# A residual chain of modulated 1-d convolutions: R's sums of the first iteration in the new order on VectorE, and the tap differences behind that iteration's tables

## The chip, the cores and the metric

The kernel runs on one core of a Trainium2 chip. The metric is the device time of one execution in microseconds (us); each kernel is run several times, and the median counts. The engines are called by the profile's names: PE is TensorE's matmul side and PEld its weight loads, DVE is VectorE, ACT is ScalarE, POOL is GpSimd, SP is SyncE, which issues most DMAs.

## The reference

A batch of 128 sequences x[b] (64 channels, 1024 positions) is run through four layers, and the result is added to x. Each layer scales its weights by a style of the batch element, normalises them (the demodulation) and convolves:

```python
def _layer(x, style, w, b, mw, mb, typ):
    s = style @ mw.T + mb
    weight = SCALE * w * s[:, None, :, None]
    demod = lax.rsqrt(jnp.sum(weight * weight, axis=(2, 3)) + EPS)
    weight = weight * demod[:, :, None, None]
    if typ == 'same':          out = conv_same(x, weight) + b
    elif typ == 'upsample':    out = blur(conv_up(x, weight) + b, 2 * k, (1, 1))
    elif typ == 'downsample':  out = conv_down(blur(x, k, (2, 2)), weight) + b
    return out
out = x
for i, typ in enumerate(('same', 'upsample', 'same', 'downsample')):
    out = _layer(out, style, weights[i], biases[i], mod_w[i], mod_b[i], typ)
return x + out
```

All weights are 64 x 64 x 3, the blur is (1, 3, 3, 1)/8, everything is float32.

## The kernel before, in words

Inside the sequence the four layers and the two blurs are one linear map from 64 to 64 channels, so the kernel multiplies the weights of all layers together for each batch element (the weight chain), and then convolves x once with the product. The batch is worked in groups of four elements, numbered q = 0 to 31: two on the two halves of the 128 partitions, times two on the free axis.

The weight chain of a group has four steps. `scale3` scales the last layer's taps (tile wd, ScalarE). `stage1` multiplies them by layer 2 into S. `stage2` multiplies S by the blurred taps E of the upsampling layer; the sums stand in PSUM as psR, and ScalarE copies them, scaled by the table tC, into R, slots 0 to 6. `stage3` multiplies R by layer 0 into Wf, the nine taps of the whole map. `combine_a` and `combine_b` then build sums of taps (tile H) on VectorE. The convolution itself is split, with such sums of taps and of input planes (tiles G and T), into five products, `conv0` to `conv4` (all at L754, into the PSUM tiles psA and Y). `sum1`, `sum2` and ScalarE's `output` put the results together, and SP's queue stores them. G and T come from the loaded planes X: `in_g01`, `in_g2`, `in3` and `in04` on VectorE, `in1` and `in2` on GpSimd for most groups.

The order of work is written out by hand. Every engine takes its instructions strictly in the order of the program text, and waits at the first one whose operands are not there. A preparation and four `early_turn`s (q = 0 to 3) come first; from q = FIRST = 4 on, `turn_of(q)` is used to near the end, and three groups are finished by hand. Turn q finishes group q and prepares n = q + 1 (combinations, first products), c = q + 2 (stages 2 and 3) and s = q + 4 (stage 1). The turn q = 4, the entry, has an order of its own, since it takes over from the early turns. The turns also carry small work at fixed places, in the lists EXTRA (early turns), TABLES and SIDE (later turns): tables of scales for the groups that follow, bias vectors, the ends of the sequences.

In `turn_of`, stage 3 is in two halves. `stage3_b` has seven products into the next psA; the last of them reads the slots 7 and 8 of R, which are two sums of other slots of R and are made by `r_sums` (L587 to L589). Its result goes by ScalarE to psW and to Wf. `stage3_a` has the other products, into psW, some of them with differences of taps in the place of taps.

From q = 5 on, stage 2 of group q + 3 is begun by `share` and finished a turn later in `stage2_rest`, which reads differences of E's taps (Ed, which lie in the tile wsq). `tap_differences` (L454 to L459) makes these with three GpSimd subtractions, once, in the list EXTRA at the end of turn 3. GpSimd's next work is the `r_sums` of turn 4, and behind it turn 4's tables, `table_C`, `vector_c2` and `vector_Da`.

Of the kernel before, what the change touches and what calls it, by code (L numbers as in the profile page):

```python
# [63 lines left out]
def kernel(  # L64
# [18 lines left out]
    nc_v, nc_a, nc_g = nc.vector, nc.scalar, nc.gpsimd  # L83
# [191 lines left out]
    def table(eng, t, bs, upper, lower, src, mul):  # L275

        qs = slice(bs.start // 4, bs.stop // 4)
        for rows, sel in ((T, upper), (Bo, lower)):
            sel = sel if isinstance(sel, tuple) else (sel,)
            n = 2 // len(sel)  # L280
            for i, s in enumerate(sel):
                v = src.rearrange("c (q s) -> c q s", s=4)[rows, :, s]
                dst = t[rows, qs, n * i : n * (i + 1)]
                if isinstance(mul, float):
                    eng.tensor_scalar_mul(dst, v, mul)
                else:
                    m = mul.rearrange("c (q s) -> c q s", s=4)[rows, :, s]
                    eng.tensor_mul(dst, v, m)
# [16 lines left out]
    def table_C(bs, eng=nc_g):  # L305
        table(eng, tC, bs, slice(0, 2), slice(2, 4), dm[:, 1, bs], dm[:, 0, bs])

    def table_3(bs):
        table(nc_g, t3, bs, ALT, ODD, dm[:, 3, bs], var[:, 3, bs])
        table(nc_g, td, bs, slice(0, 2), slice(2, 4), dm[:, 3, bs], 1.0)  # L310
# [143 lines left out]
    def tap_differences():  # L454

        d = Ed[:, :4].rearrange("c (a b) o -> c a b o", a=2)
        for b in range(2):
            nc_g.tensor_sub(d[:, :, b], E[:, 4 * b : 4 * b + 5 : 4], E[:, 2:7:4])  # L458
        nc_g.tensor_sub(Ed[:, 4:], E[:, 3:8:4], E[:, 5:6].to_broadcast([P, 2, C]))  # L459
# [62 lines left out]
    def stage2(q, pool=None, engs=(nc_a, nc_a), between=None):  # L522
        st = chain[q]
        shared = q in shared_ps
        ps = stage2_rest(q) if shared else unit(pool or ps_w, f"psR{q}")
        for n, e in enumerate(() if shared else (-2, -1, 0, 1, 2, 3, 4, 5, 6)):
            if e % 2 == 0:
                a, lo, m = slice(1, 4), e // 2 + 1, 3
            else:
                a, lo, m = slice(4, 6), (e + 3) // 2, 2  # L530
            for r, rows in enumerate(HALF):
                for c, cols in enumerate(HALF):
                    src = st[c if r == 0 else 1 - c]
                    nc.tensor.matmul(  # L534
                        ps[r][cols, lo * C : (lo + m) * C],
                        E[rows, e + 2, :],
                        src[rows, a, :],
                        start=(n == 0),
                        stop=(n == 8),
                        skip_group_check=True,  # L540
                    )
        if between:
            between()
        t = r_pool.tile([P, 2, 9, C], F32, tag="R", name=f"R{q}")
        for r in range(2):
            scaled_copy(engs[r], flat(t[:, r, :7]), ps[r][:, : 7 * C], tC[:, q, r : r + 1])
        chain[q] = t
        return ps
# [35 lines left out]
            src = ps[r][:, : n * C].rearrange("c (a o) -> c a o", o=C)  # L584
            scaled_copy(engs[r], W[:, at : at + n, r], src, t0[:, q, r : r + 1])

    def r_sums(q):  # L587
        t = chain[q]
        nc_g.tensor_add(t[:, :, 7:9], t[:, :, 2:6:3], t[:, :, 3:7:3])  # L589

    shared_w = {}

# [62 lines left out]
    def residual(q):  # L655

        W = Wq[q][0]
        for r in range(2):
            v = W[:, tap(1, 1), r, :]
            nc_v.scalar_tensor_tensor(v, idn3, t3[:, q, r : r + 1], v, op0=ALU.mult, op1=ALU.add)  # L660

    def sum_of(out, x, f, y, op=ALU.add):
        nc_v.scalar_tensor_tensor(out, x, f, y, op0=ALU.mult, op1=op)  # L663

    def taps(q):
        W, H_ = Wq[q]
        merged = (*(W[:, i] for i in TAPS), *(H_[:, i] for i in range(3)))
        return [t.rearrange("c g r o -> c g (r o)") for t in merged]

    def combine_a(q):  # L670

        chain.pop(q)
        a, b, c, h1, h2, h3 = taps(q)
        sum_of(h1, c, -2.0, a)
        residual(q)
        sum_of(h3, h1, 1.0 / 6.0, b)
# [52 lines left out]
    def in2(q, eng):  # L729
        if q < NQ:  # L730
            t, g = t_tile(q, "T12"), Gs[q]
            eng.tensor_sub(t[:, :, 1, :NJ], plane(g, 2), plane(g, 1))  # L732
# [10 lines left out]
    def product(q, m, ps, groups=range(K)):  # L743

        W, H_ = Wq[q]
        tag, i = SLOT[m]
        for g in groups:
            for s, rows in enumerate(HALF):
                for c, cols in enumerate(HALF):
                    if m in (0, 4):  # L750
                        w = W[rows, tap(m // 2, g), c, :]
                    else:
                        w = H_[rows, m - 1, g, c, :]
                    nc.tensor.matmul(  # L754
                        ps[s][cols, :NB],
                        w,
                        Ts[q, tag][rows, c, i, g : g + NB],
                        start=(g == 0 and m == 3),
                        stop=(g == K - 1),
                        skip_group_check=True,  # L760
                    )
# [42 lines left out]
    def conv2(q, *groups):  # L804
        product(q, 2, banks(q), groups or range(K))

    def sum2(q, steps=(0, 1)):
        if 0 in steps:
            m3 = m3c.pop(q)
            for s, a in enumerate(banks(q)):  # L810
                sum_of(Y[:, s, :NB], m3[:, s], 3.0, a[:, :NB])
        for s, a in parts(q) if 1 in steps else ():
            nc_v.tensor_sub(y1w[q][:, s], y1w[q][:, s], a)  # L813

    def conv4(q, *groups):
        product(q, 4, Y_banks, groups or range(K))

    def conv0(q, *groups):
        product(q, 0, banks(q), groups)
# [60 lines left out]
    def vector_Da(bs):  # L880
        nc_g.tensor_mul(Da[:, bs], sc[:, 3, bs], dm[:, 2, bs])

    def with_bias(dst, v, l, bs):
        n = bs.stop - bs.start
        nc_g.tensor_mul(dst[:, bs], v[:, bs], bb[:, l : l + 1].to_broadcast([P, n]))

    def vector_c0(bs):
        with_bias(c0f, dm[:, 1], 0, bs)
# [4 lines left out]
    def vector_c2(bs):  # L893
        with_bias(c2f, sc[:, 3], 2, bs)
# [318 lines left out]
    REST = PART[2]  # L1213
# [32 lines left out]
    def layers(i, j):  # L1246
# [11 lines left out]
            table_0(REST),  # L1258
            vector_b1(REST),
            vector_c0(REST),  # L1260
            tap_differences(),
        ),
    }


    TABLES = {
        4: lambda: (table_C(REST), vector_c2(REST), vector_Da(REST)),
        5: lambda: table_3(REST),
        6: zeros,
    }  # L1270
# [30 lines left out]
    def side(work, q):  # L1301
        work.get(q, lambda: None)()
# [111 lines left out]
    def turn_of(q):  # L1414
        n, c, s = q + 1, q + 2, q + 4
        entry = q == FIRST
        stage2(c)
        if entry:
            sum2(q)
            conv4(q)  # L1420
            r_sums(c)
        else:
            conv2(q)
            r_sums(c)
            sum2(q)
            in2(n, nc_g)
        side(TABLES, q)
        for i in range(3):
            load(c + 1, slice(i, i + 1))
        stage3_b(c, open_a(n))  # L1430
        combine_a(n)
        if entry:
            conv0(q, 0, 1)
        else:
            conv4(q)
        stage3_a(c)
        combine_b(n)
        conv3(n)
        if entry:
            copy_m3(n)  # L1440
        outputs(q, 2)
        if s < NQ:
            stage1_a(s)
        if not entry:
            copy_m3(n)
        in04(n)
        if sharing(q):
            share_sums(c + 1)
        in_g2(c)
        side(SIDE, q)  # L1450
        if q in SMALL:
            l, bs = SMALL[q]
            nc_v.memset(high(bs.stop - bs.start), 0.0)
        conv0(q, *((2,) if entry else range(K)))
        if entry:
            conv1(n, 0, 1)
        outputs(q, 1)
        if s < NQ:
            stage1_b(s)
        in_g01(c)  # L1460
        if sharing(q):
            share(c + 1, banks(q))
            share_copy(c + 1)
        outputs(q, 0)
        if q in SLOTS:
            matmuls, width, rest = SLOTS[q]
            slot(matmuls, width, Y_banks)
            rest()
        if s == NQ:
            slot(ends3, 3, unit(ps_w, "psE"), 3)  # L1470
            rest3()
        if q in SMALL:
            small(q)
        conv1(n, *((2,) if entry else range(K)))
        sum1(n)
        in3(c)
        side(LATE, q)
        if s == NQ:
            in04(c)
        in1(c, nc_g)  # L1480
        if s + 1 < NQ:
            scale3(s + 1)
# [6 lines left out]
    q, n, c = NQ - 3, NQ - 2, NQ - 1  # L1489
# [32 lines left out]
    q, n = NQ - 2, NQ - 1  # L1522
# [22 lines left out]
    q = NQ - 1  # L1545
# [90 lines left out]
```

## Time and the profile before

| | |
|---|---|
| median of 3 runs | 486.84 us (484.39 to 487.66) |
| profiled execution | 485.29 us, its span 483.5 us |
| mean granted TensorE clock | 0.994 of full |
| moved to and from HBM | 70.70 MB, mean 146 GB/s |
| GpSimd's r_sums (L589) | 25 times, 0.73 us each (median), first at 97.9 us |

The span goes from the first to the last instruction in the trace; the profiled execution's time is 1.8 us longer. The first four turns and the preparation take up to about 90 us, the turn q = 4 lies between about 89 and 108 us, and the later turns follow each other at some 14 us. In the profile, rows of a chain give start, duration and work; rows of a timeline give start, duration, engine, line, operation, output and inputs with their shapes, and in brackets how long the engine stood idle before it and for whom.

### The profile page before, as it was taken

What the parts mean: (1) busy time and instruction counts of PE and PEld (TensorE: products, weight loads), DVE (VectorE), ACT (ScalarE), POOL (GpSimd) and SP (SyncE); (2) the same over time, 40 slices, a digit from 0 to 9 for tenths busy, and PEclk for the clock granted to TensorE, in tenths of its full rate; (3) what the DMA queues carried; (4) which work ended last, traced back from release to release, by engine and by line L of the source; (5) the groups of instructions that cost most, each with busy time, mean ns of one, the idle gap of its engine ahead of it and who ended that gap; (6) DMA issues with size and microseconds to landing.
All of it is one profiled execution on the core that took longest, in us unless ns stands there. A gap on an engine that the chain in (4) does not pass through costs nothing.

```text
span 483.5 us, 26719 instructions
## 1 busy us (share of the span) xinstructions
PE 472.4 (98%) x11928; PEld 350.3 (72%) x11928; DVE 417.6 (86%) x688; ACT 310.1 (64%) x708; POOL 163.9 (34%) x198
## 2 busy tenths in 40 slices
PE   8999999889999999999999999999999999999995
PEld 7977788657887976777776777766887779776652
DVE  4899998829889999799988799988989999999895
ACT  5465666456667777567767567666666777766442
POOL 2434132735445232333322343322334323243200
PEclk9999999989999999999999999999999999999999
DMA  7215364515555454455444455443555454445225
GB/s 242 57 58 202 111 205 175 148 38 171 149 178 159 125 165 146 134 165 175 150 132 136 141 158 178 136 153 106 171 149 177 140 157 152 147 149 166 71 90 189
DMA packets 50514, 70.70 MB, mean 146 GB/s; under 512 B 5664, under 2 KB 47328, under 8 KB 50400
## 3 DMA queue, kind: packets, MB, share of 16 engines
q1 hardware_dynamic: 49808, 68.32, 45.2%
q8 instruction: 93, 1.52, 1.5%
q10 hardware_dynamic: 592, 0.69, 0.5%
q14 instruction: 21, 0.17, 0.1%
HBM read 35.36 MB, written 33.62 MB: 143 GB/s over the span
## 4 chain that ended last, share of the span: by engine, by line
PE 86%; issue 5%; POOL 4%; DVE 4%; ACT 0%; ACTq 0%; DVEq 0%; POOLq 0%
PE psA L754 41%; PE Y L754 10%; PE psR L468 9%; PE psA L572 7%; PE psW L572 6%; PE psS L390 5%; PE psR L534 3%; PE psA L468 2%; PE Y L995 2%; POOL T L732 1%; POOL T L727 1%; DVE G L663 1%; POOL wsq L458 1%; DVE H L663 1%; PE Y L337 1%
## 5 line engine op out<-in xcount | busy, mean ns | idle before, releaser
L754 PE MATMUL psA<-T,H 64*64 64x340 f32 x2304 | 186.3, 446 | 0.4 <-DVE y L663 0.2
L754 PEld LDWEIGHTS psA<-T,H 64*64 64x64 f32 x2304 | 90.8, 133 | 48.0 <-issue 2.2
L663 DVE SCALAR_TENSOR_TENSOR G<-X 128x1376 f32<-128x1376 f32 (+2 forms) x65 | 78.1, 1207 | 0.3
L446 POOL TENSOR_TENSOR S<-S 128x128 f32<-128x128 f32 x28 | 22.1, 788 | 148.8 <-ACT S L361 148.7
L727 POOL TENSOR_TENSOR T<-G 128x684 f32<-128x684 f32 x28 | 46.5, 1660 | 73.3 <-DVE G L663 70.7
L361 ACT ACTIVATE R<-psR,tC 128x448 f32<-128x448 f32 x63 | 36.5, 630 | 45.2 <-PE psR L468 25.6
L754 PE MATMUL psA<-T,Wf 64*64 64x340 f32 x768 | 65.0, 453 | 0.0
L754 PE MATMUL Y<-T,Wf 64*64 64x340 f32 x768 | 62.6, 451 | 0.1
L663 DVE SCALAR_TENSOR_TENSOR Y<-m,psA 128x340 f32<-128x340 f32 x64 | 33.1, 517 | 28.1 <-PE psA L754 26.7
L361 ACT ACTIVATE psW<-psA 128x128 f32<-128x128 f32 x100 | 19.3, 269 | 53.6 <-PE psA L572 45.1
L361 ACT ACTIVATE Wf<-psW,t 128x256 f32<-128x256 f32 (+2 forms) x76 | 32.7, 479 | 28.3 <-PE psW L572 28.0
L741 DVE TENSOR_TENSOR T<-G 128x1368 f32<-128x1368 f32 (+1 forms) x33 | 50.8, 1541 | 0.0
L712 DVE TENSOR_TENSOR T<-X 128x684 f32<-128x684 f32 x32 | 47.4, 1481 | 0.0
L468 PE MATMUL psR<-S,E 64*64 64x64 f32 (+1 forms) x1472 | 46.8, 237 | 0.0
L732 POOL TENSOR_TENSOR T<-G 128x684 f32<-128x684 f32 x28 | 46.5, 1661 | 0.0
L390 PEld LDWEIGHTS psS<-wd,w2n 64*64 64x64 f32 x1120 | 35.0, 133 | 13.7 <-ACT S L361 0.8
L468 PEld LDWEIGHTS psR<-S,E 64*64 64x64 f32 x1472 | 40.3, 134 | 4.9 <-ACT psR L491 0.2
L754 PEld LDWEIGHTS Y<-T,Wf 64*64 64x64 f32 x768 | 29.7, 132 | 17.7 <-DVE Y L663 0.7
L831 ACT ACTIVATE o<-psA,tb,td 128x340 f32<-128x340 f32 x63 | 37.0, 646 | 6.3 <-PE psA L754 6.3
L754 PEld LDWEIGHTS psA<-T,Wf 64*64 64x64 f32 x768 | 29.6, 135 | 15.4 <-issue 0.6
L831 ACT ACTIVATE o<-Y,tb,td 128x340 f32<-128x340 f32 x63 | 36.6, 637 | 4.5 <-PE Y L754 2.7
L831 ACT ACTIVATE o<-y,tb,td 128x340 f32<-128x340 f32 x62 | 38.5, 678 | 0.6 <-DVE y L813 0.6
(163 smaller groups left out, 835.6 us busy)
## 6 DMA issues: line engine op xcount, KB each, us to landing
out<-o SPq DMA_DIRECT2D x167, 170.0 KB, 2.7
X<-in_x SPq DMA_DIRECT2D x150, 172.0 KB, 3.4
X<-in_x SPq DMA_DIRECT2D x14, 516.0 KB, 5.5
out<-o SPq DMA_DIRECT2D x6, 510.0 KB, 4.5
out<-o SPq DMA_DIRECT2D x2, 340.0 KB, 2.7
Xe<-in_x_ends SPq DMA_DIRECT2D x1, 512.0 KB, 6.8
out<-o ACTq DMA_DIRECT2D x3, 170.0 KB, 2.7
par<-in_params SPq DMA_DIRECT2D x2, 192.0 KB, 3.4
```

What stands on the lines that cost most here:

```text
L361: nc_a.activation(dst, src, AF.Copy, scale=f)
L390: nc.tensor.matmul(ps[r][cols, at * C : (at + n) * C], weight[rows], wd[c if r == 0 else 1 - c][rows, taps], start=first, stop=last, skip_ ...
L446: nc_g.tensor_add(t[:, :, 2], t[:, :, 2], t[:, :, 0])
L468: nc.tensor.matmul(dst[r][cols], weight[rows], st[c if r == 0 else 1 - c][rows, slots, :], start=False, stop=last, skip_group_check=True,)
L572: nc.tensor.matmul(dst[r][cols], weight[rows], t[rows, c, slots, :], start=first, stop=last, skip_group_check=True,)
L663: nc_v.scalar_tensor_tensor(out, x, f, y, op0=ALU.mult, op1=op)
L712: nc_v.tensor_sub(t[:, pairs, 0, :NJ], plane(X, 3, pairs), plane(X, 1, pairs))
L727: eng.tensor_add(t[:, :, 0, :NJ], plane(g, 2), plane(g, 1))
L732: eng.tensor_sub(t[:, :, 1, :NJ], plane(g, 2), plane(g, 1))
L741: nc_v.tensor_sub(t[:, pairs, :, :NJ], both(a, PL), both(b, 1))
L754: nc.tensor.matmul(ps[s][cols, :NB], w, Ts[q, tag][rows, c, i, g : g + NB], start=(g == 0 and m == 3), stop=(g == K - 1), skip_group_check ...
L831: nc_a.activation(dst, src, AF.Identity, bias=add, scale=d3)
```

## The change

Three places differ. `r_sums` gets the engine as an argument: VectorE (nc_v) in the entry turn q = 4, GpSimd (nc_g) in all others. In the entry turn `combine_a(n)` stands directly behind `conv4(q)`, with `r_sums(c)` behind it, ahead of the side tables, the loads and `stage3_b`; in the other turns it stays where it was, and their order is unchanged. `tap_differences()` goes from the end of turn 3 to the end of turn 4's tables.

```diff
-    def r_sums(q):
+    def r_sums(q, eng):
         t = chain[q]
-        nc_g.tensor_add(t[:, :, 7:9], t[:, :, 2:6:3], t[:, :, 3:7:3])
+        eng.tensor_add(t[:, :, 7:9], t[:, :, 2:6:3], t[:, :, 3:7:3])
...
             table_0(REST),
             vector_b1(REST),
             vector_c0(REST),
-            tap_differences(),
         ),
...
-        4: lambda: (table_C(REST), vector_c2(REST), vector_Da(REST)),
+        4: lambda: (table_C(REST), vector_c2(REST), vector_Da(REST), tap_differences()),
...
         if entry:
             sum2(q)
             conv4(q)
-            r_sums(c)
+            combine_a(n)
+            r_sums(c, nc_v)
         else:
             conv2(q)
-            r_sums(c)
+            r_sums(c, nc_g)
             sum2(q)
             in2(n, nc_g)
         side(TABLES, q)
         for i in range(3):
             load(c + 1, slice(i, i + 1))
         stage3_b(c, open_a(n))
-        combine_a(n)
         if entry:
             conv0(q, 0, 1)
         else:
+            combine_a(n)
             conv4(q)
```

## The prediction

> **What bounds the kernel now.** I began with the page: busy time by engine, and the line of the clock that TensorE was granted in 40 slices.
>
> ```profile
> PE 472.4 (98%) x11928; PEld 350.3 (72%) x11928; DVE 417.6 (86%) x688; ACT 310.1 (64%) x708; POOL 163.9 (34%) x198
> PEclk9999999989999999999999999999999999999999
> ```
>
> TensorE (PE) is busy for 98% of the span, so time can be won only where it stands still or runs slowly. One slice of the clock, the ninth (96.7 to 108.8 us, 12.09 us a slice), is below the rest. The change lies just there, in the turn q = 4. So next came the view of waits, limited to 84 to 130 us:
>
> ```profile
> DVE Y L1453 <- ACT o L831: 7.6, 1, 7.6
> PEld psA L572 <- POOL R L589: 4.1, 1, 4.1
> PE psA L572 <- POOL R L589: 4.0, 1, 4.0
> ```
>
> L572 is a product of stage 3, L589 is GpSimd's addition in `r_sums`. TensorE waits for it once, for 4.0 us. Why the addition is late stands in the chain that ended last, from 80 to 125 us (start, duration, what):
>
> ```profile
> 94.15 0.62 POOL c0f L885
> 94.77 2.79 POOL wsq L458 x2
> 97.56 0.43 POOL wsq L459
> 97.99 0.71 POOL R L589
> 98.69 0.04 issue
> 98.74 0.59 PE psA L572 x8
> 99.33 2.27 PE psA L754 x16
> 101.60 1.19 PE psW L572 x32
> 102.78 1.72 PE psA L754 x24
> ...
> 107.52 0.04 PE Y L1238 x2
> ...
> 115.84 0.77 PE psW L572 x32
> 116.61 1.72 PE psA L754 x24
> ...
> 123.21 1.79 PE psR L468 x91
> ```
>
> The chain, on TensorE before and after, runs through GpSimd here: the tables of the turn before, then the three instructions of `tap_differences` (L458 twice, L459, 3.2 us), then `r_sums`, and only then TensorE's eight matmuls with R's sums. That GpSimd had been free to add them much earlier shows in the timelines of ScalarE and TensorE:
>
> ```profile
> 91.95 1.16 ACT L361 ACTIVATE R<-psR,tC 128x448 f32<-128x448 f32 x2 [2.30 <-PE psR L534]
> 99.43 0.77 ACT L361 ACTIVATE psW<-psA 128x128 f32<-128x128 f32 x4 [6.32 <-issue]
> 100.07 0.97 ACT L361 ACTIVATE Wf<-psA,t 128x320 f32<-128x320 f32 x2
> 94.31 0.44 PE L572 MATMUL psA<-R,w0s 64*64 64x64 f32 x16
> ```
>
> R is complete at 93.11 (91.95 + 1.16). TensorE has done all of `stage3_b` that needs no sums at 94.75 (94.31 + 0.44) and stands until 98.74: 3.99 us. ScalarE, too, stands from 93.1 to 99.4.
>
> **What the pause costs besides.** After it, 32 matmuls of the kind L572 into psW take 1.19 us; in the next turn the same 32 take 0.77 us. Small windows of the granted clock say why (the last three numbers are the clock, the DMA share and GB/s):
>
> ```profile
> 98.80:99.00 0.20, 0.20 (x8) 0.20 (x12) 0.00 (x0) 0.00 (x0) 0.16 (x1) 0.77 0.00 0
> 102.20:102.40 0.20, 0.20 (x14) 0.20 (x11) 0.00 (x0) 0.00 (x0) 0.00 (x0) 0.70 0.00 0
> 478.40:478.60 0.20, 0.17 (x4) 0.00 (x0) 0.05 (x1) 0.00 (x0) 0.00 (x0) 1.00 0.77 233
> 481.00:481.20 0.20, 0.00 (x0) 0.00 (x0) 0.00 (x0) 0.00 (x0) 0.00 (x0) 1.00 0.70 258
> 481.20:481.40 0.20, 0.00 (x0) 0.00 (x0) 0.00 (x0) 0.00 (x0) 0.00 (x0) 0.50 1.06 394
> ```
>
> A mean of 0.77 in a window that goes from 1.00 to 0.50 puts the drop at 98.91; a mean of 0.70 on the way back puts its end at 102.32. For 3.41 us TensorE ran at half clock, and lost 3.41 x 0.5 = 1.7 us of work. The other bound comes from the chain: from 98.74 to 102.78 are 4.04 us, and at full clock the same work would be 8 + 32 products at 0.77/32 and 16 at 1.72/24, that is 0.19 + 0.77 + 1.15 = 2.11 us, so 1.9 us lost. I take 1.7, as the clock itself says it; the 0.2 left over may be the filling of an empty array.
>
> **The change, part by part.**
>
> *r_sums of this turn moves to VectorE*, behind `combine_a`. One addition of 128x256 leaves GpSimd's queue (0.71 us) and one enters VectorE's. VectorE has an addition with the same operands' shape and the same kind of strided slots, L463 (first row), and these rows of its timeline lie around the new place:
>
> ```profile
> L463 DVE TENSOR_TENSOR S<-S x23: 416/418/421, 119.3 to 432.9; 128x256 f32<-128x256 f32 x23
> 92.29 0.56 DVE L663 SCALAR_TENSOR_TENSOR H<-H,Wf 128x384 f32<-128x384 f32 x1
> 92.77 0.58 DVE L663 SCALAR_TENSOR_TENSOR H<-Wf 128x384 f32<-128x384 f32 x1
> 98.13 0.67 DVE L258 SCALAR_TENSOR_TENSOR dm<-nw,dm 128x96 f32<-128x96 f32 x1
> 106.44 0.14 DVE L1453 MEMSET Y<- 128x96 f32 x1 [7.64 <-ACT o L831]
> ```
>
> `combine_a` ends at 92.85 (92.29 + 0.56). `r_sums` then waits for R, 0.26 us until 93.11, and takes 0.42: done at 93.53. At the other bound, the 0.71 us that GpSimd needed, it is done at 93.8. TensorE gets to the product at 94.75, so 0.9 to 1.2 us are in hand and the wait of 3.99 us is gone in both cases. Queued behind the waiting instruction are `combine_b`, `in04`, `in_g2` and `var_newton` (92.77 to 98.80); they come 0.8 us later and end at 99.6. The next thing on VectorE is the clearing of a strip of Y (L1453), which today waits 7.64 us for ScalarE's outputs; with everything 5.7 us earlier these are through at 100.7. So 1.1 us of cover are left, and the 0.8 us cost nothing. Without this cover they would cost up to 0.8 us.
>
> *combine_a stands ahead of the side tables, the loads and stage3_b in the text.* None of these puts anything on VectorE, so VectorE's order differs by `r_sums` alone; the loads stay on their queue in the same order. Price: nothing, and the work that hides it is not needed, as no engine's order changes.
>
> *tap_differences moves behind this turn's tables*, on GpSimd. Its three instructions and the tables keep their number:
>
> ```profile
> 98.64 0.70 POOL L288 TENSOR_TENSOR tC<-dm 64x48 f32<-64x48 f32 x2
> 99.73 0.38 POOL L881 TENSOR_TENSOR Da<-sc,dm 128x96 f32<-128x96 f32 x1
> 107.16 0.46 POOL L446 TENSOR_TENSOR S<-S 128x128 f32<-128x128 f32 x1 [7.05 <-ACT S L361]
> L458 POOL TENSOR_TENSOR wsq<-E x2: 1076/1432/1787, 94.7 to 96.5; 128x128 f32<-128x128 f32 x2
> ```
>
> The tables take 98.64 to 100.11, 1.5 us; they will start at 94.77 and end at 96.2, and the differences, 3.2 us, end at 99.5. GpSimd's next work, L446, starts at 107.16 now and so at 101.4 then: 1.9 us of cover. The differences are first read by TensorE in the second-stage products at 123.21, or 117.5 after the shift, 18 us later. Price: nothing.
>
> *What is late next.* With the sums ready, TensorE goes on at 94.75 at full clock. The eight products end about 95.0; ScalarE's four copies to psW (0.77) end at 95.9, while TensorE is in the 16 products of `conv0` until 96.1; ScalarE's two Wf copies (0.97, overlapping) end at 96.8, while TensorE is in the 32 psW products until 96.9. Each is covered by only 0.1 to 0.2 us, so up to 0.2 us may come back as waits. That cancels the 0.2 us by which the chain's price of the slow clock is above the clock's own.
>
> **Sum.** 3.99 (pause) + 1.7 (half clock) + 0 (r_sums) + 0 (differences) = 5.7 us off. The profiled execution took 485.29 us, 1.8 us more than its span of 483.5, and would take 479.6. The median of the runs is 486.84, 1.55 above it, so the forecast for a median is 486.84 - 5.7 = 481.1 us.
>
> **The rivals.**
>
> *The clock's share is not in every run (gain 4.0 us, 482.8 us).* At the end of the kernel the last matmul ends at 478.57 (478.40 + 0.17) and the clock falls at 481.20, 2.63 us later; at the pause it fell 98.91 - 94.75 = 4.16 us after the last matmul. The delay is not fixed, so the drop seems to follow a beat of its own. The two drops lie 382.29 us apart, which is 112 beats of 3.413 us, and the slow stretch was one beat long. A beat with 0.78 us of work in it (477.79 to 481.20) was followed by the drop; if that much is allowed, a pause of 3.99 us is caught in (3.99 - 2.63 + 0.78) / 3.41 = 63% of positions or more, and where the drop comes inside the pause part of the slow beat is spent idle. Between no loss and 1.7 us, most runs should lose over 1 us, and the median is near the profiled case; the chance that it is not is 0.20. The Trainium skill ("TensorE: Matmul & The Clock Gate", Part 1) has the same mechanism: a free-running window of 3413 ns that does not start with the kernel. The trace's 3.41 us and the 112 beats agree; its rule that a gap must exceed about 3.4 us would make the drop rarer than my 63% and the gain nearer to 4.0 us.
>
> *The gain is swallowed further on (486.8 us).* Something with a fixed time could come due, so that TensorE waits there instead: most likely loaded planes, or VectorE. Against it: in the pause ScalarE and VectorE run dry too, and the shift is the same for all that follows. The planes for the next turn are issued before the pause:
>
> ```profile
> 89.20 4.91 SPq L146 DMA_DIRECT2D X<-in_x  x6
> ```
>
> They leave from 89.20 on and belong to the turn behind the small product of 107.52, 101.8 after the shift. Chance 0.08, with all partial losses that leave less than 3 us.
>
> *VectorE becomes the bound of turn 4 (slower, 491.9 us).* From 93.11 it has 0.42 + 6.03 = 6.45 us of work, nearly all with two operands in SBUF beside GpSimd's tables and differences. L458 shows what such company can do: 1.08 and 1.79 us for the same size. TensorE needs the cleared strip of Y for its small product (L1238) at 107.52 - 5.7 = 101.8. If all of VectorE's stretch grew by 1.33, TensorE would begin to wait; at 2.2 the gain is gone; at 3.0 VectorE ends at 112.5, 10.8 late, and the kernel is 5.1 us slower. Against it: this stretch of VectorE lies beside a busy GpSimd today as well, and `combine_b`'s step of 384 elements takes 0.58 us, against 0.56 for `combine_a`'s. The last newton step, 0.67 us for 96 elements, does look stretched, but that is already in the 6.03. By the 1.66 of L458 the loss would be 2.1 us and the kernel still 3.6 us faster. Chance 0.06. The Trainium skill ("SBUF — State Buffer", Who interferes with whom) speaks for this rival: a VectorE instruction with two SBUF inputs and a GpSimd instruction that reads SBUF block each other. The trace agrees in part, by the 1.08 and 1.79 us of L458.
>
> **How the numbers follow.** Forecast 0.66, clock not in the median 0.20, swallowed 0.08, slower 0.06. The range goes from the lowest run less the full sum (484.39 - 5.7 = 478.7) to the highest run less the pause alone (487.66 - 4.0 = 483.7); it holds the first two cases, 0.86, less what scatter throws out. One per cent is 4.9 us, about what a measurement of this kernel can tell from no change. The forecast's 5.7 us passes it by only 0.8, so of its 0.66 I count 0.58 as faster by over 1%, and of the second case 0.07 and of the third 0.01: 0.66 faster, 0.28 within, 0.06 slower.
>
> **What would show it.** Right: R's addition on VectorE at about 93.1 and 0.42 us long; no pause of TensorE at 94.75; a clock of 1.00 through turn 4; conv3 at about 96.9 instead of 102.78; the differences from 96.2 on; the later turns as long as before. Wrong: a wait of TensorE for VectorE's R, or for L1453 at 101.8; a later turn longer than before by as much as was won.

## The result, and the profile after

The changed kernel takes 479.92 us (median of 6 runs, 478.64 to 482.59), the kernel before 485.83 us (median of 6 runs beside it, 484.39 to 487.66). The ratio is 0.9882 with a 95% interval of 0.9847 to 0.9917: 5.9 us less (4.0 to 7.4 by the interval), where 5.7 were forecast. The profiled execution took 480.28 us with a span of 478.5, 5.0 us less than that of before. Here and below, medians are of all runs, while ratios and intervals leave out the one run (489.26 us, of the control with zeros) in which the chip was in a slower state.

The page of the changed kernel, busy time and granted clock:

```profile
PE 470.0 (98%) x11928; PEld 348.4 (73%) x11928; DVE 417.8 (87%) x689; ACT 310.1 (65%) x708; POOL 162.6 (34%) x197
PEclk9999999999999999999999999999999999999998
```

One instruction has gone from GpSimd (198 before) to VectorE (688 before). The ninth slice of the clock is full; what is left is the last slice, behind the last matmul. In the waits from 84 to 125 us, TensorE's wait for R's sums is gone, and two waits of VectorE stand there in small:

```profile
DVE Y L1453 <- ACT o L831: 1.6, 1, 1.6
DVE R L589 <- ACT R L361: 0.3, 1, 0.3
```

The chain that ended last, over the same stretch as before:

```profile
92.03 1.71 PE Y L754 x24
93.74 1.33 PE psA L572 x56
95.07 1.14 PE psA L754 x16
96.22 0.77 PE psW L572 x32
96.99 1.80 PE psA L754 x24
...
101.82 0.05 PE Y L1238
...
117.51 1.96 PE psR L468 x102
```

GpSimd is no longer in it. All 56 products of `stage3_b` come in one piece, `conv0`'s 16 take 1.14 us where they took 2.27, and the 32 products into psW take 0.77 us where they took 1.19. TensorE reaches conv3 at 96.99 (102.78 before) and the second-stage products at 117.51 (123.21 before): 5.70 us earlier. VectorE in its timeline:

```profile
92.39 0.56 DVE L663 SCALAR_TENSOR_TENSOR H<-H,Wf 128x384 f32<-128x384 f32 x1
93.24 0.47 DVE L589 TENSOR_TENSOR R<-R 128x256 f32<-128x256 f32 x1 [0.29 <-ACT R L361]
98.70 0.40 DVE L258 SCALAR_TENSOR_TENSOR dm<-nw,dm 128x96 f32<-128x96 f32 x1
100.74 0.14 DVE L1453 MEMSET Y<- 128x96 f32 x1 [1.64 <-ACT o L831]
```

R's sums are done at 93.71, and TensorE comes for them about 1 us later, at 94.64 by its timeline. GpSimd in its timeline:

```profile
94.97 2.23 POOL L288 TENSOR_TENSOR tC<-dm 64x48 f32<-64x48 f32 x2
97.27 0.92 POOL L885 TENSOR_TENSOR c2f<-sc,par_s 128x96 f32<-128x96 f32 x1
98.52 0.90 POOL L458 TENSOR_TENSOR wsq<-E 128x128 f32<-128x128 f32 x2
99.38 0.45 POOL L459 TENSOR_TENSOR wsq<-E 128x128 f32<-128x128 f32 x1
101.45 0.46 POOL L446 TENSOR_TENSOR S<-S 128x128 f32<-128x128 f32 x1 [1.62 <-ACT S L361]
```

GpSimd's queue shows something that was not forecast: the table tC now takes 2.23 us (0.70 before) and c2f 0.92 (0.34), while the tap differences fall from 3.3 to 1.35 us. What stands beside VectorE's big instruction `in04` is slow in both kernels: the differences before, and now tC (`in04` runs from 95.3 to 97.0). c2f stands beside `in_g2`, VectorE's next instruction (97.1 to 98.0). The differences end at 99.83, and 1.62 us later GpSimd still waits for ScalarE.

### The profile page after: what moved, and what is told of

Same layout as the page of the kernel before. It is cut to its first block, busy times and chain, and to the rows that moved or that the text cites. A ratio compares the mean times of both kernels' runs of the same rounds, so it can differ in the third digit from the quotient of the medians.

```text
span 478.5 us, 26719 instructions
## 1 busy us (share of the span) xinstructions
PE 470.0 (98%) x11928; PEld 348.4 (73%) x11928; DVE 417.8 (87%) x689; ACT 310.1 (65%) x708; POOL 162.6 (34%) x197
## 4 chain that ended last, share of the span: by engine, by line
PE 95%; DVE 2%; DMA 1%; issue 0%; ACT 0%; SPq 0%; ACTq 0%
PE psA L754 45%; PE Y L754 11%; PE psR L468 9%; PE psA L572 7%; PE psW L572 7%; PE psS L390 6%; PE psR L534 4%; PE psA L468 2%; PE Y L995 2%; DMA par_s<-in_params_s 1%; DVE H L663 1%; PE Y L337 1%; DVE G L663 0%; PE psM L205 0%; ACT o L831 0%
## 5 line engine op out<-in xcount | busy, mean ns | idle before, releaser
L754 PE MATMUL psA<-T,H 64*64 64x340 f32 x2304 | 186.6, 447 | 0.4 <-DVE y L663 0.2
L754 PEld LDWEIGHTS psA<-T,H 64*64 64x64 f32 x2304 | 90.9, 133 | 48.1 <-issue 2.6
L754 PE MATMUL psA<-T,Wf 64*64 64x340 f32 x768 | 63.9, 446 | 0.0
L754 PE MATMUL Y<-T,Wf 64*64 64x340 f32 x768 | 62.8, 451 | 0.1
L732 POOL TENSOR_TENSOR T<-G 128x684 f32<-128x684 f32 x28 | 46.5, 1660 | 0.0
L754 PEld LDWEIGHTS Y<-T,Wf 64*64 64x64 f32 x768 | 29.7, 132 | 17.7 <-DVE Y L663 0.7
L754 PEld LDWEIGHTS psA<-T,Wf 64*64 64x64 f32 x768 | 29.1, 133 | 15.1
```

Of the source, the lines that this page charges most:

```text
L754: nc.tensor.matmul(ps[s][cols, :NB], w, Ts[q, tag][rows, c, i, g : g + NB], start=(g == 0 and m == 3), stop=(g == K - 1), skip_group_check ...
```

## The experiments

**Each part alone.** The first kernel has the tap differences behind the tables, and nothing else:

```diff
             vector_c0(REST),
-            tap_differences(),
...
-        4: lambda: (table_C(REST), vector_c2(REST), vector_Da(REST)),
+        4: lambda: (table_C(REST), vector_c2(REST), vector_Da(REST), tap_differences()),
```

> Only the tap differences move behind the tables; r_sums of turn 4 stays on GpSimd. Theory (the late sums cost the pause and a beat at half clock): the addition runs right behind c0f, from about 94.9 to 95.6, TensorE pauses about 0.8 us and keeps its full clock, so 3.99 - 0.8 + 1.7 = 4.9 us faster than before. Rival (the new engine is what matters, GpSimd is slow at its sums beside VectorE): no more than 2 us faster.

Measured: 481.88 us (median of 6) beside 485.14 for before, ratio 0.9937 (0.9916 to 0.9959), 3.3 us faster. From its timelines of GpSimd and of TensorE:

```profile
94.52 2.06 POOL L589 TENSOR_TENSOR R<-R 128x256 f32<-128x256 f32 x1
```

```profile
96.64 0.45 PE L572 MATMUL psA<-R,par 64*64 64x128 f32 x8 [2.09 <-POOL R L589]
96.91 1.32 PE L754 MATMUL psA<-T,Wf 64*64 64x340 f32 x16
```

The addition starts as early as forecast, but takes 2.06 us in place of 0.71: it now lies beside `in04`. TensorE pauses for 2.09 us, not 0.8. So the theory had the order right and the price wrong; the rival, that GpSimd is slow at its sums beside VectorE, is part of the answer, though not its bound of 2 us. The clock stayed at 1.00 through this turn in the profile. But two of the six runs, 483.45 and 484.21 us, have a mean clock of 0.995 and 0.994, below the 0.996 to 0.999 of the changed kernel's runs; the other four have 0.997 to 0.999. So the clock probably fell after this shorter pause too in those two runs; they have no trace that would show it.

The second kernel has the sums on VectorE, and the tap differences where they were:

```diff
-    def r_sums(q):
+    def r_sums(q, eng):
         t = chain[q]
-        nc_g.tensor_add(t[:, :, 7:9], t[:, :, 2:6:3], t[:, :, 3:7:3])
+        eng.tensor_add(t[:, :, 7:9], t[:, :, 2:6:3], t[:, :, 3:7:3])
...
             conv4(q)
-            r_sums(c)
+            combine_a(n)
+            r_sums(c, nc_v)
...
```

> Only r_sums of turn 4 goes to VectorE behind combine_a; the tap differences stay at the end of turn 3. Theory: TensorE no longer waits for GpSimd at all, the whole 5.7 to 5.9 us are won, no pause, and the tap differences cost nothing where they are. Rival (both parts are needed): GpSimd, held by the differences, is late with turn 4's tables, and 1 us or more is left on the table.

Measured: 479.19 us (median of 4) beside 485.14, ratio 0.9877 (0.9861 to 0.9893), 5.95 us faster. TensorE's timeline has no pause:

```profile
93.94 0.44 PE L572 MATMUL psA<-R,w0s 64*64 64x64 f32 x16
94.17 0.43 PE L572 MATMUL psA<-R,par 64*64 64x128 f32 x8
94.40 1.35 PE L754 MATMUL psA<-T,Wf 64*64 64x340 f32 x16
```

The sums on VectorE are the whole gain. Moving the differences adds nothing that these runs can tell; where they stay, the tables behind them end at 99.5, and GpSimd still waits 1.5 us for ScalarE before its next work, so the rival falls.

**The clock's share.** Products of zeros fill the pause of the kernel before:

```diff
+    def fill(n):
+        spare = unit(ps_w, "psFill")
+        for i in range(n):
+            r = i % 2
+            nc.tensor.matmul(
+                spare[r][HALF[i // 2 % 2], :NB], Z[HALF[r], :C], Z[HALF[r], :NB], start=True, stop=True
+            )
...
         for i, (at, weight, slots) in enumerate(plan):
+            if q == FIRST + 2 and i == len(plan) - 1:
+                fill(22)
             same_row(blocks(ps, at), weight, t, slots, i == 0, i == len(plan) - 1)
```

> The kernel before, with 22 products of zeros (64x340, into a free PSUM tile, some 3.1 us) put ahead of the product that waits for R's sums; the output is the same. Theory: the pause remains, TensorE goes on at 98.7 as before, but the clock stays at 1.00, so 1.7 us faster than before. Rival (the slow products after the pause come from the pause itself, not from the clock gate, or the clock falls all the same): no change, or slower by what the added products delay.

The same lines in the changed kernel were the control:

> The changed kernel with the same 22 products of zeros at the same place as in the warm-pause kernel: here they fill no pause and only cost their own time, 44 half-products at 1.72/24 us, 3.15 us. Theory (products of zeros cost their time and nothing else): 3.15 us over the changed kernel, about 483, which leaves 0.85 us of pause for the 484.4 of the warm-pause kernel. Rival (they cost more than their time, and so the warm-pause kernel showed too small a gain): 484 or above.

Measured: 484.36 us (median of 12) beside 485.14 for the warm pause, ratio 0.9978 (0.9960 to 0.9997); 483.57 (median of 8) beside 485.63, ratio 0.9944 (0.9923 to 0.9965), for the control, as its theory had it. The row of `conv0` in the timeline of the kernel before:

```profile
99.09 2.51 PE L754 MATMUL psA<-T,Wf 64*64 64x340 f32 x16
```

The warm pause's timeline of TensorE (lines that are added ahead move the numbers of the lines behind, here L754 to L765):

```profile
93.81 3.63 PE L597 MATMUL psFill<-Z 64*64 64x340 f32 x44
97.98 0.45 PE L572 MATMUL psA<-R,par 64*64 64x128 f32 x8 [0.54 <-POOL R L589]
98.25 1.32 PE L765 MATMUL psA<-T,Wf 64*64 64x340 f32 x16
```

The clock stayed full, and `conv0` behind the pause took 1.32 us, not 2.51. It took 1.32 us in the first kernel above as well, where the pause of 2.09 us was empty and the clock did not fall: it is the clock that makes these products slow, and not the standing still. The step from one turn's second sum (VectorE's subtraction y) to the next shows what that is worth without the noise of the rest. The rows of turn 3 and turn 4 in VectorE's timeline, first of the kernel before:

```profile
90.46 0.85 DVE L813 TENSOR_TENSOR y<-y,psA 128x680 f32<-128x680 f32 x1
113.75 0.85 DVE L813 TENSOR_TENSOR y<-y,psA 128x680 f32<-128x680 f32 x1
```

Of the changed kernel:

```profile
90.56 0.85 DVE L813 TENSOR_TENSOR y<-y,psA 128x680 f32<-128x680 f32 x1
108.04 0.85 DVE L813 TENSOR_TENSOR y<-y,psA 128x680 f32<-128x680 f32 x1
```

Of the warm pause:

```profile
89.73 0.85 DVE L824 TENSOR_TENSOR y<-y,psA 128x680 f32<-128x680 f32 x1
111.40 0.85 DVE L824 TENSOR_TENSOR y<-y,psA 128x680 f32<-128x680 f32 x1
```

And of the control:

```profile
91.86 0.85 DVE L824 TENSOR_TENSOR y<-y,psA 128x680 f32<-128x680 f32 x1
112.75 0.86 DVE L824 TENSOR_TENSOR y<-y,psA 128x680 f32<-128x680 f32 x1
```

The steps are 23.29, 17.48, 21.67 and 20.89 us. The change takes 5.81 us out of this step; the warm clock alone takes out 1.62, against the 1.7 forecast. The medians give the warm pause only 0.8 us, but the interval of 0.15 to 1.9 holds the 1.62. In the control the filling was forecast to cost 3.15 us; it costs 3.41 in this step, 3.65 by the medians and 3.0 by the ratios (0.9944 against 0.9882). Whether it has a price of its own in the warm pause, where it lies in time that TensorE would have stood still, these runs do not show. So the 1.6 us are shown in the trace; how much of them reaches the median is open.

**A shorter and a longer pause.** In one kernel r_sums comes between the first and the second tap difference; in the other the differences are made twice. In the first diff, the argument 0 stands for the first subtraction and 1 for the other two.

```diff
-            tap_differences(),
+            tap_differences(0),
...
-        4: lambda: (table_C(REST), vector_c2(REST), vector_Da(REST)),
+        4: lambda: (tap_differences(1), table_C(REST), vector_c2(REST), vector_Da(REST)),
```

> The kernel before, with r_sums of turn 4 between the first and the second of the three tap differences, so that TensorE's pause is 1.9 to 2.6 us in place of 4.0. Theory (a pause this short leaves too much work in each beat, the clock does not fall): clock 1.00 through turn 4, and 1.4 to 2.1 us of pause plus 1.7 of clock are won, 3.1 to 3.8 in all. Rival (the loss by the slow clock goes with the length of the pause): half of each, 2.3 to 3.0 us, and a dip of the clock in the profile.

```diff
             tap_differences(),
+            tap_differences(),
```

> The kernel before with the three tap differences made twice at the end of turn 3, so that r_sums of turn 4 is later still by 1.3 us (as beside an idle VectorE) to 3.2 us (as beside a busy one). Theory (every us on GpSimd ahead of the sums is a us of the kernel, and the clock falls in nearly every run): 1.3 to 3.2 us slower than before, up to 1.7 more where a second beat runs at half clock. Rival (the pause is partly hidden elsewhere): under 1 us.

Measured: 484.01 us (median of 12) beside 485.14 for the shorter pause, ratio 0.9983 (0.9964 to 1.0002); 486.48 (median of 11) beside 485.63 for the longer, ratio 1.0015 (0.9998 to 1.0032). The shorter one's timeline of TensorE:

```profile
98.43 0.70 PE L573 MATMUL psA<-R,par 64*64 64x128 f32 x8 [3.13 <-POOL R L590]
```

Windows of its clock (engines' busy time, then the clock, DMA share and GB/s):

```profile
97.40:97.60 0.20, 0.00 (x0) 0.00 (x0) 0.20 (x1) 0.00 (x0) 0.20 (x1) 0.93 0.00 0
94.16:97.57 3.41, 1.14 (x51) 0.99 (x41) 3.29 (x4) 0.00 (x0) 3.39 (x4) 1.00 0.31 98
97.57:100.98 3.41, 2.55 (x24) 1.47 (x28) 1.71 (x4) 1.61 (x6) 2.93 (x7) 0.50 0.00 0
100.98:104.40 3.42, 3.42 (x52) 2.26 (x48) 0.00 (x0) 0.84 (x2) 0.00 (x0) 0.50 0.03 5
104.40:104.60 0.20, 0.20 (x8) 0.13 (x4) 0.00 (x0) 0.00 (x0) 0.00 (x0) 1.00 0.00 0
```

And, for comparison, the same two beats of the kernel before:

```profile
95.50:98.91 3.41, 0.17 (x6) 0.17 (x10) 3.14 (x5) 0.00 (x0) 3.41 (x5) 1.00 0.04 13
98.91:102.32 3.41, 3.41 (x44) 2.21 (x44) 0.00 (x0) 1.61 (x6) 1.05 (x4) 0.50 0.00 0
```

Both theories for the shorter pause fall: the median is 1.1 us lower (-0.1 to 1.7), less than either had; only the dip of the clock, from the rival, came. The pause was 3.13 us, since the addition took 1.34 us beside VectorE, and the clock fell all the same: at 97.57, at the end of a beat in which TensorE had worked 1.14 of 3.41 us. The next beat, with 2.55 us of work, did not bring it back; only a full one did, at 104.40. TensorE thus worked 5.97 us at half clock and lost 3.0 us, almost as much as by the pause. In the kernel before, the beat ended 0.17 us after the pause, so the one slow beat was full of work; here it ended inside the pause. In these traces the slow clock thus costs one beat or two, by where the pause lies in the beat, and not in proportion to the pause: the step between the second sums is 23.66 us here (91.01 to 114.67), 0.37 us longer than before's, with a pause 0.86 us shorter.

Most runs of this kernel have a higher mean clock than the profiled one. A slow beat takes 3.41 x 0.5 / 484 = 0.0035 off the mean, and the slow stretch at the kernel's end takes its part as well (0.0024 in the trace of the kernel before, 2.3 us from 481.2 to 483.5). By this estimate three of the twelve runs have two slow beats (0.991 or 0.992, the profiled run among them), eight have one (0.994 or 0.995), and the fastest, 482.62 us with 0.997, has none.

The longer pause was 5.24 us, by TensorE's timeline:

```profile
100.78 0.71 PE L572 MATMUL psA<-R,par 64*64 64x128 f32 x8 [5.24 <-POOL R L589]
```

Its clock is at half from 100.0 to 106.8, two beats:

```profile
100.00:100.20 0.20, 0.00 (x0) 0.00 (x0) 0.00 (x0) 0.00 (x0) 0.20 (x2) 0.53 0.00 0
106.80:107.00 0.20, 0.20 (x8) 0.13 (x4) 0.00 (x0) 0.00 (x0) 0.00 (x0) 0.90 0.00 0
```

It is 1.25 us longer than before's, and the step between the second sums is 25.82 us (91.25 to 117.07), 2.53 us longer: the pause, and 1.28 us beyond it, with a second slow beat. But the profiled run is the slowest of the eleven, and the medians differ by 0.85 us only, with an interval from -0.1 to 1.6. That is the rival's size (under 1 us), and the interval also holds the lower end of the theory (1.3 us): the runs do not decide between them.

**How much is in hand.** In the entry turn all of `combine_b` goes ahead of the sums:

```diff
             combine_a(n)
+            combine_b(n)
             r_sums(c, nc_v)
...
-        combine_b(n)
+        if not entry:
+            combine_b(n)
```

> The changed kernel with all of combine_b ahead of r_sums on VectorE in the entry turn. r_sums then ends about 95.15 in place of 93.7, and TensorE reaches it at about 94.85. Theory (0.9 to 1.2 us are in hand, no more): a pause of 0.3 to 0.4 us, clock 1.00, time 0.3 us over the changed kernel, too little for the median. Rival (VectorE's order does not matter here): no pause in the profile.

Measured: 480.62 us (median of 4), ratio to before 0.9884 (0.9859 to 0.9909). VectorE's timeline, and TensorE's:

```profile
95.06 0.56 DVE L589 TENSOR_TENSOR R<-R 128x256 f32<-128x256 f32 x1
```

```profile
95.68 0.45 PE L572 MATMUL psA<-R,par 64*64 64x128 f32 x8 [0.35 <-DVE R L589]
```

The pause is 0.35 us, as forecast: `combine_b`'s 1.7 us is more than the cover.

**VectorE in every turn.** If VectorE is the better place once, is it always?

```diff
-            r_sums(c, nc_g)
+            r_sums(c, nc_v)
```

> The changed kernel with r_sums on VectorE in all 25 turns, not in the entry turn alone. Theory (GpSimd is off the path in the later turns, and VectorE has about 0.5 us between R and the first sum2): no change against the changed kernel, 479.5 to 480.5. Rival (VectorE, 87% busy, becomes the bound): 0.4 us more in each of 24 turns, up to 10 us slower than the changed kernel.

Measured: 496.99 us (median of 4) beside 485.63 for before, ratio 1.0221 (1.0196 to 1.0247): 17 us slower than the changed kernel, more than the rival allowed. My theory fell. The instruction (count, shortest, median and longest in ns):

```profile
L589 DVE TENSOR_TENSOR R<-R x25: 417/1377/1862, 94.1 to 451.2; 128x256 f32<-128x256 f32 x25
```

The wait of TensorE that it makes (us, times, longest):

```profile
PEld Y L754 <- DVE Y L663: 15.5, 21, 0.8
```

And GpSimd's `in2` in the groups (busy us, mean ns):

```profile
L732 POOL TENSOR_TENSOR T<-G 128x684 f32<-128x684 f32 x28 | 59.0, 2109 | 0.0
```

The two meet, for example, in these rows of the timelines of GpSimd and VectorE:

```profile
121.11 2.27 POOL L732 TENSOR_TENSOR T<-G 128x684 f32<-128x684 f32 x1
122.66 1.01 DVE L589 TENSOR_TENSOR R<-R 128x256 f32<-128x256 f32 x1 [0.77 <-ACT R L361]
```

The sums take 1.38 us in the median instead of 0.42, and GpSimd's `in2` (L732) 2.11 in the mean instead of 1.66. While r_sums was on GpSimd, it held `in2` back until R was there; without it `in2` runs into VectorE's sums, these delay `sum2`, and TensorE waits for Y. To tell this from VectorE's wait for R, `in2` was put behind the sums again, by a tiny copy:

```diff
+    after_r = const.tile([P, 2], F32, name="after_r")
...
             r_sums(c, nc_v)
+            nc_g.tensor_copy(after_r, chain[c][:, 0, 8, :2])
```

> As the kernel with r_sums on VectorE in all turns, but with a copy of two columns of R's sums on GpSimd ahead of its in2, so that in2 can't start before the sums are done. Theory (VectorE's sums and GpSimd's in2 stand in each other's way, 1.38 against 0.42 us and 2.27 against 1.65 us): the sums take 0.42 to 0.5 us again, and most of the 17 us come back, 480 to 485. Rival (the loss comes from VectorE waiting for R ahead of sum2, whoever runs beside it): 490 or more.

> The changed kernel once more, on the chip of the run before, as its control: 479 to 481.

Measured: 480.31 us (median of 4) and, for the control, 479.43 (median of 4), both beside 486.05; ratios 0.9875 (0.9852 to 0.9899) and 0.9866 (0.9842 to 0.9890). The sums with the tiny copy, and `in2` in the groups:

```profile
L589 DVE TENSOR_TENSOR R<-R x25: 410/425/461, 95.2 to 435.9; 128x256 f32<-128x256 f32 x25
```

```profile
L733 POOL TENSOR_TENSOR T<-G 128x684 f32<-128x684 f32 x28 | 46.5, 1661 | 0.0
```

With the two apart, both have their old times and all but 0.9 us of the loss is gone. The 25 sums together take 10.6 us, where they took 30.0. VectorE waits for R as before, 13.6 us in 22 turns here against 9.9 us in 21, so the rival falls: it was the meeting of the two engines, not VectorE's load or its wait for R. None of these versions beats the changed kernel or its sums alone.

## Why the prediction was right

- *The sum*: 5.7 us forecast, 5.9 measured, with an interval of 4.0 to 7.4. That the two are so close is in part luck: the profiled pair gained 5.0 us, and one term was too small as a mean (below). The median itself was forecast at 481.1 us and is 479.92; 1.0 of the 1.2 us between them is the kernel before, whose median is 485.83 us with three more runs and was 486.84 with three.
- *The pause* (3.99 us): gone entirely. The place on VectorE behind `combine_a`, the wait for R (0.26 forecast, 0.29 measured) and the length (0.42, measured 0.47) came out; the cover of about 1 us is borne out by the kernel with late sums.
- *The half clock* (1.7 us): the warm pause gives 1.62 in the trace. But 1.7 was the loss at one position of the pause in the beat. 42 runs of the kernel before in two groups have mean clocks of 0.994 to 0.996 (26 runs), of 0.993 or less (15) and of 1.000 (one); over all 0.9937, against 0.998 in the changed kernel's six. The difference of 0.0043 on 483.5 us is 2.1 us, an upper estimate, since half clock costs nothing while TensorE stands still. So the term was up to 0.4 us too small as a mean, and 3.99 + 2.1 = 6.1 stands beside the 5.9 measured. The times of the runs speak for somewhat less: the 15 took 486.12 us in the median and the 26 took 485.11, so a second slow beat costs some 1.0 us. By the mean clocks 41 of the 42 runs had a drop, where the prediction's working gave 63% or more: it let a beat hold no more than 0.78 us of work, and the shorter pause shows a drop after 1.14 us. This speaks against the first rival, that the clock's share is not in most runs; the interval of the times alone, with its lower end of 4.0 us, would not exclude it.
- *The 0.2 us left over* (set to 0): the prediction's other bound for the half clock, 1.9 us, lies 0.2 above the 1.7. These 0.2 us are a cost of a pause at full clock too: with the pauses of 0.35 and 2.09 us the step between the second sums is 18.07 us (91.03 to 109.10) and 19.81 us (90.25 to 110.06), 0.24 us more than their length above the 17.48 of the changed kernel. So 3.99 + 1.6 + 0.24 account for the 5.81 us of this step. The prediction set the 0.2 us off against waits behind the pause, and these did not come. That the 0.2 us are the filling of an empty array, no run shows.
- *combine_a and the differences* (0 us): right, as the kernel with the sums alone shows. The working was not: tables and differences were to end at 96.2 and 99.5, and ended at 98.6 and 99.8, since now the tables lie beside `in04`.
- *What is late next*: conv3 was forecast at 96.9 and came at 96.99; the covers of ScalarE held.
- *VectorE as the bound of turn 4*: it did not happen there; VectorE even ended earlier than forecast (99.1 against 99.6) and the cover ahead of L1453 was 1.64 us, not 1.1. The mechanism is real, though: with the sums on VectorE in all turns it cost 17 us. The Trainium skill ("SBUF — State Buffer", Who interferes with whom) has the rule that a VectorE instruction with two SBUF inputs and a GpSimd instruction that reads SBUF contend; the runs agree, with 0.42 to 1.38 us on the one side and 1.66 to 2.11 on the other.
- *Swallowed further on*: no. The 5.7 us are there at 117.5; of the profiled pair 5.0 are left at the end, and of the medians 5.9. Later turns differ by a few tenths either way; why is open.

## What to carry to other kernels

An engine that is busy for a third of the time can still be late at one place: look at what stands ahead of the one instruction that others wait for, and move that instruction to an engine that is free just then. In these traces TensorE's pauses of 3.1 to 5.2 us cost 1.8 to 3.1 us more than their length, most of it by half clock, and pauses of 0.35 and 2.09 us only 0.24 us more. And before a step is moved off a queue, ask what it held back there: on GpSimd the sums kept `in2` away from VectorE, and without that they cost 17 us.

## What the hardware showed that was not expected

The clock fell in a pause of 3.13 us as well, at the end of a beat with a third of work in it (1.14 of 3.41 us), and a beat with three quarters (2.55 us) did not bring it back. The Trainium skill ("TensorE: Matmul & The Clock Gate", HAM oscillation) gives as a rule that pauses over about 3.4 us are to be avoided; by these rows 3.1 us is too long already, and the loss after it was 3.0 us. By the mean clocks of two runs, a pause of some 2.1 us may be too long at times. And the same addition of 128x256 on GpSimd took 0.73 us beside VectorE's last two Newton steps, 1.34 beside `in_g2` and the first Newton step, and 2.06 beside `in04`.
